# Six blocks instead of three by seven products of quarters, and side work in larger steps

## The chip, the cores and the metric

The program runs on one core of one Trainium2 chip. The metric is the device time of one execution in microseconds (us), the median of the runs shown. Beside it stands one profiled execution, whose span runs from its first to its last instruction. The engines are named as in the profile: PE is TensorE (matmuls), PEld its loads of the stationary operand, DVE is VectorE, ACT is ScalarE, POOL is GpSimd and SP is SyncE, which issues DMAs.

## What is computed

The input x has 4 sequences of 1024 tokens of 256 values, all in float32. Three layers follow one another:

```python
def ffn(x):                                   # weights w1 .. w3 hold -1, 0 and 1
    h = silu(lin(x, w1, s1)) * lin(x, w2, s2)       # 256 -> 1024
    h = gelu(lin(h, h1, s3)); h = gelu(lin(h, h2, s4))   # 1024 -> 1024, twice
    return lin(h, w3, s5)                           # 1024 -> 256
x = x + 0.5 * ffn(layernorm(x))
x = x + gelu(causal_convolution(layernorm(x), K)) @ W.T + b
x = x + 0.5 * ffn(layernorm(x))                # the same weights
```

K is a convolution kernel of 1024 taps for each of the 256 channels, computed from the inputs with exponentials, sines and cosines. The convolution goes over a Fourier transform of 2048 points.

## The kernel before

**Blocks.** The feed-forward network runs over 16 blocks of 512 tokens: f0 to f7 for the first application, g0 to g7 for the second. In a block there are first the two narrow layers w1 and w2 (64 matmuls of 512 columns, lines L382 and L383), then the two *wide* layers h1 and h2 (128 each, L415), then w3 (32, in `last_squares`, L630; in the last block in `last_tokens`, L658). An activation is split into a high and a low part (`fp32r`, a format of fewer bits that TensorE multiplies faster than float32), and the weights are whole numbers, so two matmuls make one exact product. The splitting costs a copy on ScalarE (L420) and a subtraction on VectorE (`low_part`, L309) for each tile.

**By quarters.** The last `N_BY_SUMS` blocks compute the wide layers in another way (`winograd`, L518). Both operands are cut into 2 x 2 quarters, and seven products of quarters take the place of eight, by the scheme of Strassen and Winograd. Each product is 32 pairs of stationary and moving tiles in `product` (L477) with 256 moving columns, twice for the two parts; so a wide layer is 224 matmuls of 256 columns. Sums and differences of activations are made on VectorE (`less`, `plus`), every operand is split (`operand`, L460), and the seven weight sums come from DRAM: `weight_sums` (L584) makes them once for both layers, in 16 parts of two VectorE operations each, and stores them. `load_slot` (L576) brings one of them, 1 MB, into one of four slots through SP's queue whenever a product is done. The slots take the SBUF space of the wide weights; so before the first such block all mixes and all parts of the weight sums have to be finished (L1285 to L1294: what is left of the sums is issued there in one go, and an assertion holds that the last mix is through).

**Side work.** Everything else runs beside the matmuls of the wide layers, given out in small steps by a generator, `all_aside` (L1225): the taps and their spectrum (`kernel_steps`, `kernel_spectrum`), then four *mixes*, m0 to m3 (`mix`, L1046), each the convolution of one sequence. Mix b needs blocks f(2b) and f(2b+1); blocks g(2b) and g(2b+1) need mix b. A mix has matmuls of its own on TensorE (L966, L1144, L1169). A second generator, `fillers` (L1244), holds the 16 parts of the weight sums and then 44 `weight_checks`: each loads 256 KB of weights again, compares them with -1, 0 and 1 (ScalarE's Sign for h1 and h2) or with the weights held, and counts misses; where one is found, a whole second version of the network runs, which it does not for these inputs.

**The counter.** `tick` (L1249) runs after each of the 16 output tiles of the wide layers but the last, 15 times in a block (in a block by quarters at 15 of 28 half products). It adds `STEP_WORK` (from f7's end on `STEP_WORK_2`) to an allowance and takes steps of `all_aside` until what they have issued reaches it. `counted` (L150) charges each of their VectorE operations `OP_WORK` = 130 plus its columns; a step without such an operation is charged `MIN_WORK` = 300. A step can also yield `PAUSE`: what comes next needs something that is still under way, so the tick ends there and the rest of its allowance is lost. At a pause one step of `fillers` is taken, if more than 642 of the allowance is left and `done` has more than eight entries (it has from f4 on). `prepare` (L1195) normalizes and transposes the next block's input in between; its VectorE operations are charged too, 4,900 in a block.

**Order on the engines.** Within these limits the instructions of an engine are put into an order when the program is built: the earliest written one that is ready comes first. A late operand at the start of a layer can thus be bridged by matmuls of the next output tiles. PSUM has eight tiles of a bank each (`psum`, L143), SBUF tiles of half a block come from a ring of 19 (`half`, L168), split operands from one of 15 (`ring`, L172).

Of the kernel before, what the change touches and what calls it, by code (L numbers as in the profile page):

```python
# [24 lines left out]
TB = 512  # L25
# [9 lines left out]

STEP_WORK, STEP_WORK_2, OP_WORK, MIN_WORK = 2500, 3000, 130, 300
PAUSE = "pause"
N_CHECKS = 44  # L40

N_BY_SUMS = 3
QT = TB // 2
QK = KH // 2
QW = HID // 2
# [62 lines left out]
def macaron_layers(  # L110
# [37 lines left out]
    work_done = 0  # L148
# [213 lines left out]
    def linear(ps, w, m, acts):  # L362
        n = len(acts)
        for k in range(n):
            for part in range(parts):
# [6 lines left out]
                )  # L372

    def ffn(xt, src, dst, blk, name, tick, ahead, final, by_sums):


# [21 lines left out]
        for layer, w in ((2, h1_sb), (3, h2_sb)):  # L398
            if by_sums:
                at = 0  # L400

                def step():
                    nonlocal at
                    at += 1
                    if at * KH // 14 > (at - 1) * KH // 14:
                        ahead()
                        if layer == 2 or at < 14:
                            tick()

                raw = winograd(raw, layer, name, step)  # L410
                continue
            hb = []
            for m in range(KH):
                ps = bank(f"p{layer}_{name}_{m}")
                linear(ps, w, m, ha)  # L415
                t = ring(f"h{layer}_{name}_{m}", parts, TB, dtype=wide)
                g = half(f"g{layer}_{name}_{m}") if split else t[:, 0, :]
                nc.scalar.activation(g, ps, AF.Gelu, scale=sc_sb[:, layer, m : m + 1])  # L418
                if split:
                    nc.scalar.copy(t[:, 0, :], g)  # L420
                    low_part(t, g)
                hb.append(t)
                ahead()
                if layer == 2 or m < KH - 1:
                    tick()
            ha = hb
# [91 lines left out]
    def winograd(raw, layer, name, step):  # L518
# [51 lines left out]
        (quarters[layer][i], f"w_{n}_{layer}_{i}")  # L570
        for n in range(N_BY_SUMS)
        for layer in range(2)
# [620 lines left out]
    done = []  # L1193
# [50 lines left out]
    fillers = chain(sums_of_weights, checks) if split else iter(())  # L1244
    late = late_pool = None
    ticks = 0
    allowed = 0

    def tick():  # L1249


        nonlocal ticks, allowed, work_done
        ticks += 1
        allowed = min(allowed, work_done) + (
            STEP_WORK_2 if ("f", n_blocks - 1) in done else STEP_WORK
        )
        while work_done < allowed:
            at = work_done
            if next(aside, PAUSE) is PAUSE:
                if len(done) > 8 and allowed - work_done > OP_WORK + TB:  # L1260
                    next(fillers, None)
                break
            if work_done == at:
                work_done += MIN_WORK
# [8 lines left out]
    allowed = work_done  # L1273
    for n, (turn, blk) in enumerate(blocks):
# [8 lines left out]

        by_sums = split and n >= len(blocks) - N_BY_SUMS
        if by_sums and not slots:  # L1285
# [93 lines left out]
```

## Time and profile before

| | us |
|---|---|
| median of 3 runs | 1400.81 (1399.09 to 1400.86) |
| the profiled execution | 1398.44 |
| its span | 1396.7 |
| TensorE busy / VectorE busy / ScalarE busy | 1384.2 / 932.8 / 766.8 |
| clock granted to TensorE, share of full speed | 0.999 |

The main groups of matmuls, by line (columns: line, engine, operation, output <- inputs, partitions x elements and how many; then busy us, mean ns of one, idle us of the engine before them):

| line | what | number | busy us |
|---|---|---|---|
| L366 | wide layers of 13 plain blocks (p_f, p_g) | 3328 of 512 columns | 768.4 |
| L366 | narrow layers of 16 blocks (pa, pb) | 1024 of 512 columns | 274.7 |
| L484 | wide layers of 3 blocks by quarters | 1344 of 256 columns | some 12.1 for each 96 |
| L630, L658 | w3 | 416 of 512 and 192 of 256 columns | 121.8 |
| L893, L966, L1144, L1169 | taps, spectra, mixes | | 115.2 |

A matmul's mean duration (391 ns for 512 columns) is longer than the distance to the next one (227 ns), since matmuls overlap; so distances and stretches of time are read here rather than durations. The same holds in a smaller way on VectorE, whose operations of 0.685 us overlap a little.

### The profile page before, as it was taken

To read this page: it belongs to the slowest core of one execution; us is meant where nothing else is said; L and a number is where in the kernel's file an instruction comes from. 1 tells how busy PE (TensorE), PEld (TensorE's weight loads), DVE (VectorE), ACT (ScalarE), POOL (GpSimd) and SP (SyncE) were. 2 spreads that over 40 slices of the span, in tenths; PEclk is the share of its full clock that TensorE was granted. 3 is DMA by queue.
4 is the path that set the end of the run, shared out by engine and by line. 5 is a ranking of instruction groups with operands and counts; after the bars stand their busy time and mean duration, and the time that the engine had idled before them with its cause. 6 is when DMAs were issued, how large, how long until landed. Compare 5 with 4: busy or idle time off the path is not lost.

```text
span 1396.7 us, 19695 instructions
## 1 busy us (share of the span) xinstructions
PE 1384.2 (99%) x7132; PEld 1182.6 (85%) x7132; DVE 932.8 (67%) x1766; ACT 766.8 (55%) x1227; POOL 297.0 (21%) x454
## 2 busy tenths in 40 slices
PE   9999999999999999999999999999999999999998
PEld 7888888888888888888888888888888888989998
DVE  6896667755637776377774569844597536877765
ACT  5986579644546445354353544534544445766664
POOL 4441022211312121521125301221112032121200
PEclk9999999999999999999999999999999999999999
DMA  9430101113131331532314414233132356959663
GB/s 355 127 131 21 41 16 46 31 30 96 50 108 36 106 90 54 203 92 83 76 46 162 134 37 128 61 91 106 53 95 50 100 143 237 332 169 320 193 221 114
DMA packets 121677, 160.11 MB, mean 115 GB/s; under 512 B 73873, under 2 KB 84113, under 8 KB 116193
## 3 DMA queue, kind: packets, MB, share of 16 engines
q1 hardware_dynamic: 99296, 99.41, 23.5%
q0 software_dynamic: 22000, 59.07, 13.7%
q8 instruction: 58, 0.95, 0.3%
q14 instruction: 51, 0.41, 0.1%
q10 hardware_dynamic: 272, 0.26, 0.1%
HBM read 120.95 MB, written 37.75 MB: 114 GB/s over the span
## 4 chain that ended last, share of the span: by engine, by line
PE 93%; DVE 3%; DMA 2%; ACT 1%; issue 0%; POOL 0%; SPq 0%; DVEq 0%; POOLq 0%; ACTq 0%
PE p_f L366 31%; PE p_g L366 19%; PE pa_f L366 4%; PE pa_g L366 4%; PE pb_f L366 4%; PE pb_g L366 4%; PE po_f L630 4%; PE po_g L630 4%; PE p2a_g L484 3%; PE p3a_g L484 3%; PE pi L1144 2%; PE pw L1169 2%; PE pf_m L966 2%; PE p2d_g L484 1%; PE p3d_g L484 1%; PE pk L893 1%
## 5 line engine op out<-in xcount | busy, mean ns | idle before, releaser
L366 PE MATMUL p_f<-h_f,h_sb 128*128 128x512 f32 x1024 | 237.1, 391 | 0.0
L366 PE MATMUL p_f<-ha_f,h_sb 128*128 128x512 f32 x1024 | 235.3, 390 | 0.0
L366 PEld LDWEIGHTS p_f<-h_f,h_sb 128*128 128x128 f32 x1024 | 191.8, 188 | 40.0 <-DVE h_f L309 0.3
L366 PEld LDWEIGHTS p_f<-ha_f,h_sb 128*128 128x128 f32 x1024 | 191.9, 188 | 39.8
L418 ACT ACTIVATE g_f<-p_f,sc_sb 128x512 f32<-128x512 f32 x128 | 87.7, 689 | 190.5 <-PE p_f L366 186.0
L309 DVE TENSOR_TENSOR h_f<-g_f,h_f 128x512 fp32r<-128x512 f32 x128 | 87.7, 689 | 143.3 <-ACT h_f L420 142.9
L418 ACT ACTIVATE g_g<-p_g,sc_sb 128x512 f32<-128x512 f32 x80 | 55.2, 690 | 174.6 <-PE p_g L366 165.0
L366 PE MATMUL p_g<-ha_g,h_sb 128*128 128x512 f32 x640 | 148.1, 391 | 0.0
L366 PE MATMUL p_g<-h_g,h_sb 128*128 128x512 f32 x640 | 147.9, 391 | 0.1
L366 PEld LDWEIGHTS p_g<-h_g,h_sb 128*128 128x128 f32 x640 | 120.0, 188 | 25.4 <-ACT h_g L420 0.5
L366 PEld LDWEIGHTS p_g<-ha_g,h_sb 128*128 128x128 f32 x640 | 120.0, 188 | 24.7
L309 DVE TENSOR_TENSOR h_g<-g_g,h_g 128x512 fp32r<-128x512 f32 x80 | 55.2, 690 | 111.8 <-ACT h_g L420 111.3
L339 POOL DMA_DIRECT2D moved<-sq_g x64 | 34.9, 552 | 314.9 <-DVE sq_g L156 313.8
L420 ACT CAST h_f<-g_f 128x512 fp32r<-128x512 f32 x128 | 78.3, 618 | 2.9
L418 ACT ACT_TABLE_LOAD x46 | 59.0, 1283 | 20.9 <-PE p_f L366 12.4
L366 PE MATMUL pa_f<-xt_f,w_sb 128*128 128x512 f32 x256 | 69.0, 390 | 0.7 <-DVE xt_f L321 0.7
L366 PE MATMUL pb_f<-xt_f,w_sb 128*128 128x512 f32 x256 | 68.8, 389 | 0.0
L366 PE MATMUL pa_g<-xt_g,w_sb 128*128 128x512 f32 x256 | 68.5, 389 | 0.0
L366 PE MATMUL pb_g<-xt_g,w_sb 128*128 128x512 f32 x256 | 68.4, 389 | 0.0
L392 DVE SCALAR_TENSOR_TENSOR g_g<-pb_g,sc_sb,g_g 128x512 f32<-128x512 f32 x64 | 47.7, 748 | 29.9 <-PE pb_g L366 19.2
L339 POOL DMA_DIRECT2D moved<-sq_f x56 | 30.8, 556 | 159.1 <-DVE sq_f L156 159.1
L392 DVE SCALAR_TENSOR_TENSOR g_f<-pb_f,sc_sb,g_f 128x512 f32<-128x512 f32 x64 | 47.3, 746 | 23.0 <-PE pb_f L366 15.9
(310 smaller groups left out, 2493.9 us busy)
## 6 DMA issues: line engine op xcount, KB each, us to landing
w<-q SPq DMA_DIRECT2D x42, 1024.0 KB, 6.1
q<-s POOLq DMA_DIRECT2D x40, 256.0 KB, 3.4
h_sb<-in_h_dram POOLq DMA_DIRECT2D x8, 1024.0 KB, 14.6
given<-in_h_dram SPq DMA_DIRECT2D x32, 256.0 KB, 5.0
kr<-k_hat SPq DMA_DIRECT2D x20, 256.0 KB, 2.7
ki<-k_hat SPq DMA_DIRECT2D x20, 256.0 KB, 2.9
xr_f<-in_x_dram SPq DMA_DIRECT2D x64, 64.0 KB, 2.5
q<-h_sb POOLq DMA_DIRECT2D x16, 256.0 KB, 5.8
```

The source lines that it names most:

```text
L309: return nc.vector.tensor_tensor(t[:, 1, :], src, t[:, 0, :].bitcast(F32), ALU.subtract)
L339: stores.dma_start(moved[k].rearrange("(c r) a q -> a r c q", r=SQ)[a], sq[a * SQ : (a + 1) * SQ].rearrange("r c j s -> r c (j s)"),)
L366: nc.tensor.matmul(ps, w[:, k, m * P : (m + 1) * P], acts[k][:, part, :], start=(k == 0 and part == 0), stop=(k == n - 1 and part == parts ...
L392: nc.vector.scalar_tensor_tensor(g if split else t[:, 0, :], pb, sc_sb[:, 1, m : m + 1], g, ALU.mult, ALU.mult)
L418: nc.scalar.activation(g, ps, AF.Gelu, scale=sc_sb[:, layer, m : m + 1])
L420: nc.scalar.copy(t[:, 0, :], g)
L484: nc.tensor.matmul(ps[:, e * QT : (e + 1) * QT], weights[:, c, m * P : (m + 1) * P], ops[c // 2][:, part, c % 2 * QT : (c % 2 + 1) * QT], ...
L630: nc.tensor.matmul(ps[:, n * n_t : (n + 1) * n_t], w3_sb[:, k, o * P : (o + 1) * P], act(k, part, n * n_t, (n + 1) * n_t), start=(k == ord ...
L893: nc.tensor.matmul(pk[0:NA, at + i, :, :].rearrange("p h b -> p (h b)"), a[:, i].rearrange("p a b -> p (a b)"), qd[d1 // per_tile][:, at + ...
L966: nc.tensor.matmul(ps[e][:, part, :], m[:, e, part, :], rows_of(q + JQ * e), start=True, stop=True)
L1144: nc.tensor.matmul(banks[dc][e][:, q * P : (q + 1) * P], vs[q + JQ * e][:, part, dc * P : (dc + 1) * P], m[:, e, part, :], start=(part == ...
L1169: nc.tensor.matmul(ps[:, e * D : (e + 1) * D], yts[dc][j // JQ][:, (j % JQ + e) * P : (j % JQ + e + 1) * P], wt_sb[:, dc, :], start=(dc == 0),
```

## The change

Three edits. `N_BY_SUMS` goes from 3 to 6: blocks g2, g3 and g4 are computed by quarters too, and everything that has to be through before the first such block, the last mix and the sums of the weights, has to be so before g2 instead of g5. The steps of side work become larger, 3600 for 2500 and 4000 for 3000. And at a pause up to two steps of `fillers` are taken, each under the same condition, instead of one.

```diff
-STEP_WORK, STEP_WORK_2, OP_WORK, MIN_WORK = 2500, 3000, 130, 300
+STEP_WORK, STEP_WORK_2, OP_WORK, MIN_WORK = 3600, 4000, 130, 300
...
-N_BY_SUMS = 3
+N_BY_SUMS = 6
...
             if next(aside, PAUSE) is PAUSE:
-                if len(done) > 8 and allowed - work_done > OP_WORK + TB:
-                    next(fillers, None)
+                for _ in range(2):
+                    if len(done) > 8 and allowed - work_done > OP_WORK + TB:
+                        next(fillers, None)
                 break
```

## The prediction

> **What bounds the kernel.** I read the page's busy shares and its chain of waits first, then busy time by stretches of time, one stretch per block of the feed-forward network.
>
> ```profile
> PE 1384.2 (99%) x7132; PEld 1182.6 (85%) x7132; DVE 932.8 (67%) x1766; ACT 766.8 (55%) x1227; POOL 297.0 (21%) x454
> ...
> PE 93%; DVE 3%; DMA 2%; ACT 1%; issue 0%; POOL 0%; SPq 0%; DVEq 0%; POOLq 0%; ACTq 0%
> ```
>
> TensorE is busy 1384.2 of 1396.7 us, and some 9 us of the rest are its start. So only two things move the end: fewer or shorter matmuls, or a new wait on TensorE. The stretches show both sides (start, length, then each engine's busy time with its instructions, clock, DMA share, GB/s):
>
> ```profile
> 9.20:89.60 80.40, 80.35 (x353) 66.04 (x354) 66.83 (x165) 67.01 (x91) 27.01 (x47) 1.00 0.72 231
> 89.60:176.00 86.40, 86.40 (x450) 71.65 (x449) 59.11 (x109) 52.09 (x89) 17.17 (x26) 1.00 0.13 31
> 440.90:520.70 79.80, 79.80 (x354) 66.09 (x353) 60.03 (x107) 38.05 (x56) 15.30 (x24) 1.00 0.33 90
> 795.50:882.60 87.10, 87.04 (x386) 71.97 (x384) 70.61 (x141) 41.43 (x62) 13.62 (x21) 1.00 0.31 85
> 1157.40:1237.60 80.20, 78.05 (x578) 73.97 (x577) 59.67 (x110) 56.26 (x107) 12.85 (x20) 1.00 0.81 283
> 1237.60:1313.80 76.20, 76.20 (x579) 73.52 (x579) 57.28 (x107) 50.67 (x96) 13.44 (x21) 1.00 0.73 241
> 1313.80:1390.00 76.20, 76.15 (x578) 73.43 (x576) 49.05 (x77) 48.23 (x91) 8.89 (x11) 1.00 0.45 157
> ```
>
> These are blocks f0, f1, f5, g1 and the three by quarters, g5 to g7. A plain block without side matmuls takes 79.8 us (f5), one by quarters 76.2 (g6, g7), and g5, the first of them, 80.2 because its TensorE stands still for 2.15 us. VectorE reaches 83% in f0 and 81% in g1 with no stall of TensorE.
>
> **Part 1: g2, g3, g4 by quarters.** Each exchanges 256 matmuls of 512 columns for 448 of 256 in the two wide layers, and 32 for 64 behind them. The wide layers alone, plain (f7) and by quarters (g6, g7):
>
> ```profile
> 636.00:694.00 58.00, 58.00 (x257) 48.06 (x256) 43.70 (x74) 22.13 (x34) 6.62 (x12) 1.00 0.33 90
> ...
> 1252.10:1306.10 54.00, 54.00 (x451) 53.83 (x450) 42.71 (x83) 39.65 (x77) 5.47 (x10) 1.00 0.84 291
> 1328.40:1382.30 53.90, 53.90 (x451) 53.90 (x450) 36.24 (x58) 37.33 (x74) 0.00 (x0) 1.00 0.57 205
> ```
>
> That is 4.0 us less there; the last layer gives back some 0.4 (64 narrow matmuls in 7.7 us against 32 wide ones in 7.3). Block against block: 79.8 - 76.2 = 3.6 us, three times **-10.8 us**.
>
> Here a rule of the Trainium skill stands against the row. "TensorE: Matmul & The Clock Gate", section "Back-to-back issue gap", gives N/2.4 + 2.5 ns for N columns: 215.8 and 109.2 ns, so 55.2 against 48.9 us, 6.3 saved per block and 18.9 in all. The section "LDWEIGHTS" of the same page speaks against that, and against the change: a stationary load costs columns/1.2, 107 ns for 128, about as long as a stream of 256, so nothing hides it. The rows side with the second: weight loads fill 53.90 of 53.90 us by quarters (48.06 of 58.00 before), and a step is 54.0/448 = 120 ns, not 109. I take 3.6 per block; no faster VectorE or DMA would improve it.
>
> The new blocks also add VectorE and ScalarE work. g7, nearly without side work, holds 49 and 48 us of 76.2, so both are covered. Each needs 14 weight parts of 1 MB, 184 GB/s over 76.2 us. g6 moved 241 GB/s with no stall, g5 283 with one; without the checks' loads the new blocks stay below g6. The first four parts cannot start before g1's last read of the wide weights, and have the last layer and the first one, some 22 us, until needed. g5 had the same start.
>
> **The stall in g5** (2.15 us by the row, 4.0 by the pitch) coincides with 15 weight checks there, whose DMAs share the rate above: on ScalarE the row of the sign operation waits 5.2 us for them in all, and the last layer waits for its operands:
>
> ```profile
> L630 PE MATMUL po_g<-hl_g,w_sb 128*128 128x256 f32 x128 | 16.6, 286 | 1.5 <-ACT hl_g L465 1.1 <-DVE hl_g L309 0.4
> ```
>
> After the change no check is left for these blocks (below). The gain is between 0 (a first block by quarters stalls anyway) and 4.0; I take **-3**, as g6 and g7 with few or no checks show none.
>
> **Part 2: larger steps.** The counter charges 130 plus its columns for a VectorE operation. 642 units are one 512-wide operation of 0.685 us (mean of the row of y<-y,z), 1.07 ns a unit; but operations in a row overlap by some 0.07 us, so in busy time it is less. At 0.94 f5's row (60.0 us, 37.5 thousand units with preparation) leaves 25 us for the block's own work, which is what its groups add up to (8 x 0.747 + 24 x 0.7 + two transposes and the input's split = 26). I take 0.94 and keep 1.07 as the upper end. I replayed the rule tick by tick over the unchanged list of steps: kernel taps and spectrum 129 thousand units, four mixes of 59, weight sums 16 x 1284, checks 44 x 642. Mix b still waits for f(2b+1). Units in thousands per block, without preparation (4.9 each):
>
> f0 33 to 49; f1 30 to 49; f2 34 to 34; f3 26 to 46; f4 26 to 36; f5 33 to 45; f6 33 to 44; f7 31 to 38; g0 30 to 50; g1 39 to 20; g2 to g7 together 100 to 0.
>
> The last mix ends at tick 144, six before g2's start at 150; the sums of weights are through in f6. So nothing is left to run in bulk at the exchange of pools. Nor does TensorE's side work grow: the same products come earlier.
>
> What grows is the load of VectorE and ScalarE. **f0:** VectorE 66.8 + 16.6 x 0.94 = 82.4 us against 80.4 of TensorE; **f1:** 59.1 + 19.3 x 0.94 = 77.2 against about 80 + 8 (half the tap products). **g0:** 25 + 55.1 x 0.94 = 77 (85 at 1.07) against 80 + 7 (forward products of mix 3). So f0 is over-full, f1 and g0 are nearly full, and f3, f5 and f6 lie below 93% at either price. ScalarE in f0:
>
> ```profile
> L418 ACT ACT_TABLE_LOAD x10 | 12.8, 1283 | 0.2
> ```
>
> That is ten reloads for Gelu in f0's wide layers (58.2 us), and as many for Exp, Sin and Sqrt. The first tap group's functions now all fall into f0: about six switches and four functions more. The Trainium skill, "ScalarE: Activation LUTs", section "What ACT_TABLE_LOAD costs", counts 1.28 us plus 1.38 of drain. By that six more switches cost 16 us, 86 of 80.4, and f0 would be late by 5 or more on ScalarE alone; the row shows 0.2 us of idle time before ten loads, so no drain, and I take 6 x 1.28 + 4 x 0.7 = 10.5: 67.0 + 10.5 = 77.5, nearly full.
>
> What of this reaches TensorE? In f0 of before the splits of h (L309) end up to 6.6 us after their matmuls and TensorE loses 0.1 us: the program's PE order fills in other matmuls while the last split is late. Ends: 0 if the excess drains in the 22 us without ticks that each block has; and the whole excess of the ticks, side + own split 0.69 + preparation against 3.63 us of matmuls and the side matmuls: f0 0.5 x 15 = 8 (14 at 1.07), g0 0 to 8, f3 0 to 3, f1 0 to 6. Sum 8 to 31. I take less than the lower sum, since f0 and f1 together need 160 of 168 us and each layer end tolerates 6.6: f0 3, f1 1, g0 1, **+5 us**.
>
> **Part 3: two fillers at a pause.** Same operations, only closer. A second check uses data whose load was issued just before; 3.6 us to landing (median, g0 to g4) can hold ScalarE, with Gelu behind it. Eight PSUM banks cover it except at a layer's end. A pair of weight sums queues seven stores of 0.55 us on POOL before the next block's squares; POOL is busy 21%. Between 0 and 5; I take **+1**.
>
> **Sum.** -10.8 - 3 + 5 + 1 = -7.8: span 1388.9, with the 1.7 us around it 1390.6 for the profiled run's 1398.4. The median shown lies 2.4 above that run: 1393.
>
> **Rivals.** A, *backlog reaches TensorE* (slower): VectorE's queue, f0 and g0 above all, is paid at layer ends. Price 8 to 31, taken 25, since it is a rival only at 1.07 ns a unit: 1400.8 - 13.8 + 25 = 1412; it decides once the stalls pass 14 us. For it: f0's 82.4 against 80.4. Against it: 81 to 83% cost nothing, and the full blocks have slack ones behind them. B, *a draw*: g2 stalls as g5 did and the stalls are near 11: 1400.8 - 10.8 + 11 = 1401, or 1398 to 1403. C, *no new wait*: 1400.8 - 13.8 = 1387. D, that three more blocks don't become cheaper, has g6 and g7 against it and I give it nothing.
>
> **Chances.** Forecast 0.59, A 0.21, B 0.13, C 0.07. 0.2% is 2.8 us, about what this measurement can tell: faster 0.66, same 0.13, slower 0.21. The range takes in C, the forecast, B and the edge of A: 1386 to 1405.
>
> **What would show it.** g3 to g7 at 76.2 us each; g2 at 76 (else the g5 stall was not the checks); TensorE's gaps in f0, f1 and g0 summing to about 5 us, ended by VectorE's splits or ScalarE; no checks after tick 144. Wrong if gaps beyond 14 us stand at layer ends, or if a tile that is not free holds Gelu up.

## The result and the profile after

| | before | after |
|---|---|---|
| median of 12 runs each, us | 1400.18 (1398.27 to 1401.11) | 1396.53 (1393.47 to 1400.46) |
| ratio, 95% interval | | 0.9975 (0.9967 to 0.9983) |
| the profiled execution / its span, us | 1398.44 / 1396.7 | 1396.3 / 1394.3 |

The change makes the kernel 3.65 us faster, of the 7.8 us that were forecast. The page of the changed kernel, its busy times and the first line of its chain of waits:

```profile
PE 1376.4 (99%) x7804; PEld 1205.9 (86%) x7804; DVE 1012.3 (73%) x1886; ACT 795.2 (57%) x1336; POOL 296.4 (21%) x454
...
PE 40%; DVE 3%; issue 0%; DVEq 0%
```

TensorE is busy 7.8 us less, by coincidence the sum that was forecast, but the span is only 2.4 us shorter: the difference is new idle time. The chain adds up to 43%, so it could be followed back over the last part of the program only; it is no ground for anything about the first half, where most side work is.

The stretches of the blocks f0, f1, g3 and g7 (start:end, length, busy time with instructions of PE, PEld, DVE, ACT and POOL, granted clock, DMA share, GB/s):

```profile
9.20:91.10 81.90, 81.86 (x352) 67.16 (x353) 72.89 (x169) 67.60 (x92) 29.19 (x51) 0.98 0.69 220
91.10:182.60 91.50, 89.79 (x482) 73.21 (x482) 76.97 (x137) 66.46 (x112) 15.48 (x24) 1.00 0.09 21
931.90:1007.80 75.90, 75.90 (x577) 73.41 (x576) 53.21 (x81) 48.35 (x92) 13.50 (x21) 1.00 0.79 270
1311.70:1387.80 76.10, 76.09 (x578) 73.37 (x576) 49.63 (x76) 48.23 (x91) 8.93 (x11) 1.00 0.46 157
```

The third line is one of the new blocks by quarters: 75.9 us, TensorE without a gap. The first two are the heavily loaded ones. (What the splitting is for shows in the distances of matmuls with 256 columns: 120 ns in `fp32r` by quarters, 216 ns in float32 in the mixes.)

**An account of the lost time.** Since busy time hides part of a stall (matmuls overlap), the loss is taken from starts: the distance between two matmuls in succession, less the usual distance of their kind (227 ns for 512 columns, 120 for 256), summed per block. Blocks with less than 0.9 in both are left out of the table.

| us lost | f0 | f1 | f2 | f3 | f4 | f7 | g0 | g1 | g5 | all blocks |
|---|---|---|---|---|---|---|---|---|---|---|
| before | 1.3 | 0.9 | 0.9 | 1.5 | 0.4 | 0.3 | 0.5 | 0.7 | 4.25 | 13.3 |
| after | 2.9 | 3.8 | 1.5 | 0.4 | 0.9 | 1.5 | 7.85 | 2.7 | 0 | 22.4 |

So the three blocks gave 10.8 or a little more, g5 gave back 4.25, and the other blocks took 13.4: -10.8 - 4.25 + 13.35 = -1.7, against -2.4 in the spans (with 79.8 - 75.9 = 3.9 us a block it is 11.7, and the sum -2.6). Of the new loss, 9.3 us lie in one place, the last layer of g0 and the start of g1's first layer. TensorE there, in the timeline (start, length, engine, line, operation; in brackets the idle time before and what ended it):

```profile
821.00 5.15 PE L630 MATMUL po_g<-h_g,w_sb 128*128 128x512 f32 x22
827.98 0.73 PE L630 MATMUL po_g<-h_g,w_sb 128*128 128x512 f32 x2 [1.83 <-DVE h_g L309]
829.41 1.22 PE L630 MATMUL po_g<-h_g,w_sb 128*128 128x512 f32 x2 [0.70 <-ACT h_g L420]
833.40 2.07 PE L630 MATMUL po_g<-h_g,w_sb 128*128 128x512 f32 x4 [2.77 <-DVE h_g L309]
```

The first 22 matmuls of w3 use tiles that are split already; the other ten come in small groups, whenever a split of h arrives. By starts the three waits are 2.0, 0.9 and 3.2 us, together 6.0. And the engines in stretches of 5 us through g0's second wide layer and its end:

```profile
786.00:791.00 5.00, 5.00 (x24) 4.14 (x23) 2.20 (x5) 1.31 (x2) 0.00 (x0) 1.00 0.56 149
796.00:801.00 5.00, 5.00 (x22) 3.86 (x22) 5.00 (x9) 2.83 (x5) 3.49 (x7) 1.00 0.33 85
806.00:811.00 5.00, 5.00 (x23) 4.13 (x23) 4.93 (x20) 3.42 (x6) 1.10 (x2) 1.00 0.69 220
816.00:821.00 5.00, 5.00 (x24) 4.13 (x22) 5.00 (x10) 1.74 (x4) 0.00 (x0) 1.00 0.41 125
826.00:831.00 5.00, 2.10 (x5) 0.80 (x4) 5.00 (x10) 1.89 (x3) 0.00 (x0) 0.76 0.00 0
831.00:836.00 5.00, 2.60 (x6) 1.66 (x6) 5.00 (x10) 2.01 (x3) 0.00 (x0) 0.50 0.53 84
```

The third busy number is VectorE: full from some 791 to 836 us, while ScalarE (the fourth) has 1.3 to 3.4 us in 5. So VectorE is behind. The splits of this layer end 5.1, 4.8, 11.0, 12.5, 13.4, 14.0, 15.8 and 15.0 us after the last matmul of their tiles, where before they ended 2.1 to 3.5 us after. From the third tile on, 7.4 to 10.5 us of this lie ahead of Gelu, which waits for VectorE to free a tile (below), and the rest behind it, in VectorE's own queue.

The two last lines also show a lower granted clock, 0.76 and 0.50 on average. In stretches that end where it changes, it is full, then half, then full again:

```profile
826.00:828.50 2.50, 0.67 (x3) 0.30 (x2) 2.50 (x6) 0.48 (x1) 0.00 (x0) 1.00 0.00 0
828.60:838.80 10.20, 6.74 (x15) 4.30 (x15) 9.80 (x23) 4.11 (x8) 0.00 (x0) 0.50 0.34 54
838.90:841.00 2.10, 2.10 (x11) 1.72 (x10) 2.10 (x6) 2.07 (x3) 0.36 (x1) 1.00 0.00 0
```

Twelve matmuls stand 400 to 600 ns apart in the middle stretch, which is 3.0 of the 9.3 us.

### The profile page after: what moved, and what is told of

Same layout as the page of the kernel before. It is cut to its first block, busy times and chain, and to the rows that moved or that the text cites. A ratio compares the mean times of both kernels' runs of the same rounds, so it can differ in the third digit from the quotient of the medians.

```text
span 1394.3 us, 21329 instructions
## 1 busy us (share of the span) xinstructions
PE 1376.4 (99%) x7804; PEld 1205.9 (86%) x7804; DVE 1012.3 (73%) x1886; ACT 795.2 (57%) x1336; POOL 296.4 (21%) x454
## 3 DMA queue, kind: packets, MB, share of 16 engines
q0 software_dynamic: 22000, 59.07, 13.5%
## 5 line engine op out<-in xcount | busy, mean ns | idle before, releaser
L366 PE MATMUL p_f<-ha_f,h_sb 128*128 128x512 f32 x1024 | 238.8, 392 | 0.1
L392 DVE SCALAR_TENSOR_TENSOR g_g<-pb_g,sc_sb,g_g 128x512 f32<-128x512 f32 x64 | 47.4, 746 | 29.4 <-PE pb_g L366 23.8
L391 ACT ACTIVATE g_g<-pa_g,sc_sb 128x512 f32<-128x512 f32 x64 | 43.6, 688 | 42.1 <-PE pa_g L366 41.9
L630 PE MATMUL po_f<-h_f,w_sb 128*128 128x512 f32 x256 | 60.7, 391 | 1.6 <-ACT h_f L420 0.9
L366 PE MATMUL p_g<-ha_g,h_sb 128*128 128x512 f32 x256 | 59.8, 392 | 0.0
L366 PEld LDWEIGHTS pa_f<-xt_f,w_sb 128*128 128x128 f32 x256 | 48.8, 190 | 12.2 <-DVE xt_f L356 1.0
L366 PE MATMUL p_g<-h_g,h_sb 128*128 128x512 f32 x256 | 59.1, 391 | 0.0
L630 PEld LDWEIGHTS po_f<-h_f,w_sb 128*128 128x128 f32 x256 | 47.6, 188 | 13.0 <-DVE h_f L309 2.0
L418 ACT ACTIVATE g_g<-p_g,sc_sb 128x512 f32<-128x512 f32 x32 | 22.1, 690 | 62.4 <-PE p_g L366 43.1
```

The lines of the kernel that those rows point to most:

```text
L366: nc.tensor.matmul(ps, w[:, k, m * P : (m + 1) * P], acts[k][:, part, :], start=(k == 0 and part == 0), stop=(k == n - 1 and part == parts ...
L391: nc.scalar.activation(g, pa, AF.Silu, scale=sc_sb[:, 0, m : m + 1])
L392: nc.vector.scalar_tensor_tensor(g if split else t[:, 0, :], pb, sc_sb[:, 1, m : m + 1], g, ALU.mult, ALU.mult)
L630: nc.tensor.matmul(ps[:, n * n_t : (n + 1) * n_t], w3_sb[:, k, o * P : (o + 1) * P], act(k, part, n * n_t, (n + 1) * n_t), start=(k == ord ...
```

## The experiments

The question was which part of the change makes this loss. The theories: **the step** (4000 units put more on VectorE in this layer than it can take beside the matmuls); **the pair of fillers** (a pair of checks put down at one pause blocks ScalarE or VectorE); **the ring** (VectorE is late with tiles of half a block, ScalarE's Gelu waits for one to come free, and this, not VectorE's own speed, makes the split late). A fourth, **the exchange** of memory pools before g2, could move the loss with the number of blocks by quarters.

**A smaller second step alone.**

```diff
-STEP_WORK, STEP_WORK_2, OP_WORK, MIN_WORK = 3600, 4000, 130, 300
+STEP_WORK, STEP_WORK_2, OP_WORK, MIN_WORK = 3600, 3000, 130, 300
```

> The changed kernel with the second step at 3000 instead of 4000 (first 3600, two fillers, six blocks). By the counter g0 then takes 39 thousand units instead of 50 and g1 31 instead of 20; the last mix ends at tick 148, still before g2. Theory 1 (VectorE is over-full in g0's second wide layer, and its backlog reaches TensorE there): the 9.8 us that TensorE loses at g0's end go, and the half clock behind them; time 8 to 10 us below the changed kernel, near 1387, ratio to before 0.990 to 0.992. Theory 2 (the pairs of checks hold ScalarE and VectorE): g0 and g1 keep five and six pairs, so at most a third of the loss goes, near 1393 to 1396. Theory 3 (Gelu waits for one of the 19 half tiles, which VectorE frees late): as theory 1, since with a shorter queue the tiles come free sooner; this run does not part the two.

(The 9.8 us there are an earlier count of the 9.3 above.)

Measured: 1392.01 against 1399.01, ratio 0.9956 (0.9942 to 0.9969). The loss at g0's end is 0.1 us. That is the step, and not the pair or the blocks, which were left as they are. It gained less than it removed, since the checks now reach into g1 (4.7 us lost) and a late split costs 1.4 us in g3. One wait in g1 is of a kind that I had not thought of. From the timeline of this kernel:

```profile
904.21 1.04 DVE L309 TENSOR_TENSOR h_g<-g_g,h_g 128x512 fp32r<-128x512 f32 x1 [3.38 <-ACT h_g L420]
...
907.83 0.69 DVE L309 TENSOR_TENSOR h_g<-g_g,h_g 128x512 fp32r<-128x512 f32 x1 [1.97 <-ACT h_g L420]
908.44 0.19 DVE L731 TENSOR_REDUCE total<-miss 128x1 f32<-128x44 f32 x1
...
908.78 0.19 PE L734 MATMUL p_bad<-ones,total 128*1 128x1 f32 x2 [2.35 <-DVE total L731]
```

The last step of the checks sums the misses by a matmul of one column. In TensorE's order it stands ahead of the layer's next matmuls, and TensorE stands still 2.4 us for it. VectorE isn't full there: it is idle for 3.4 and 2.0 us, since in its order two splits of h, each waiting for ScalarE's copy, stand ahead of the sum. Behind the wait the clock is at half for 3.4 us, and seven matmuls cost 1.4 us more; together 3.9 of g1's 4.7.

**One filler at a pause.**

```diff
-                for _ in range(2):
+                for _ in range(1):
```

> The changed kernel with one filler at a pause instead of two (steps 3600 and 4000, six blocks). g0's second layer keeps its 3852 to 5778 units a tick; some 24 checks move behind g1, into g2 to g4, one in a tick. Theory 1: g0's end still loses 8 to 10 us, time within 2 us of the changed kernel where g2 stalls by nothing, up to 4 us above it if g2 then stalls as g5 did before (checks and weight parts share the DMA rate). Theory 2: the loss at g0's end goes, 6 to 10 us below the changed kernel.

Measured: 1405.23 against 1399.01, ratio 1.0043 (1.003 to 1.0057), some 9 us slower than the change: a miss. The loss at g0's end stays at some 7 us, so a pair is worth at most some 2 of it. But with one filler at a time the checks aren't through before g2, and g2 loses 12.0 us. Its stretches (columns as above) and the waits around it (engine, output, line, what it waited for; us, times, longest):

```profile
960.00:975.00 15.00, 14.82 (x121) 14.35 (x119) 11.58 (x23) 10.37 (x23) 2.18 (x4) 1.00 0.93 301
975.00:990.00 15.00, 12.04 (x97) 11.62 (x96) 7.52 (x15) 7.01 (x13) 3.31 (x6) 1.00 0.94 343
990.00:1005.00 15.00, 10.47 (x66) 10.18 (x67) 11.12 (x21) 10.69 (x22) 0.00 (x0) 0.77 0.57 224
```

```profile
ACT sign L714 <- DMA given<-in_h_dram: 11.3, 4, 5.0
PEld p3a_g L484 <- ACT t3s_g L465: 5.3, 1, 5.3
```

The DMA engines are at 0.94, the checks' loads and the parts of the weights of the first block by quarters share them; ScalarE's sign waits 11.3 us for four of these loads, 5.0 for one. What stands behind it in ScalarE's order, and behind the comparison in VectorE's, comes late, and TensorE waits 5.3 us for its operand. g5's stall before was of this kind, a third as large.

**The blocks undone.**

```diff
-N_BY_SUMS = 6
+N_BY_SUMS = 3
```

> The changed kernel with three blocks by quarters as before: only the larger steps and the second filler. No gain from g2 to g4. Theory 1: the stalls of f1, f6 and g0 and the rest (some 14 us more than before) remain, and the 4 us lost in g5 before go, since no check is left there: time 8 to 11 us above before, ratio 1.006 to 1.008. If the stalls at g0's end come from the exchange of pools behind g1 or from the earlier weight parts, they are gone here and the time is 2 to 5 us below before.

Measured: 1405.86 against 1399.01, ratio 1.005 (1.0037 to 1.0064). Against the change's 0.9975 that is 0.75%, or 10.5 us for three blocks, where 10.8 were forecast. The loss at g0's end is 8.3 us with three blocks as well, with g2's start and its exchange far away; the exchange isn't the cause.

**One more tile in the ring, and its control.** The ring of 19 gets a twentieth tile. Two constants had to become narrower to make room for it, so the control has these alone.

```diff
-        return work.tile([P, *(shape or (512,))], dtype, tag="half", name=name, bufs=19)
+        return work.tile([P, *(shape or (512,))], dtype, tag="half", name=name, bufs=20)
...
-    miss = keep.tile([P, P], F32, name="miss")
+    miss = keep.tile([P, N_CHECKS], F32, name="miss")
...
-    eps = small.tile([P, 1 + 88], F32, name="eps", bufs=1)[:, 0:1]
+    eps = small.tile([P, 1], F32, name="eps", bufs=1)
```

> The changed kernel with 20 half tiles instead of 19 (the space comes from two constants that were wider than needed). Theory 3 (Gelu is held because no half tile is free): one tile more lets Gelu run further ahead of VectorE; g0's loss falls by a quarter or more, 2 to 5 us less. Theory 1 (VectorE's own rate; the waiting for a tile only passes it on): the split of h behind Gelu is as late as before, and the time stays within 1.5 us of the changed kernel.

> The changed kernel with the two narrower constants of d_half20 and 19 half tiles as before: the same instructions, only later SBUF addresses of the tiles behind them, not a multiple of what they were. d_half20's 512-column matmuls followed each other at 233 ns instead of 227 and it took 20 us more. If the addresses do that, the distance is 232 to 233 ns here too for the layers concerned, 15 to 28 us above the changed kernel, and its stalls say nothing against d_half20's reading. If the twentieth tile did it, the distance stays at 227 and the time is that of the changed kernel.

Measured: with 20 tiles 1415.98 against 1399.01, ratio 1.0117 (1.0102 to 1.0133); the control 1413.96 against 1399.7, ratio 1.0103 (1.0088 to 1.0119). Both are 18 to 20 us slower than the change, for a reason that has nothing to do with the ring (see the last section). But the stall can be compared: 8.8 us at g0's end with 20 tiles, 8.4 with 19, and the splits of the layer are late by the same 4.8, 4.7, 10.8, 12.2, 13.0, 13.5, 15.2 and 14.3 us in both. ScalarE's Gelu around that layer, in the change (797 to 828 us) and then with 20 tiles (815 to 850 us; groups: line, engine, operation, count, then busy us, mean ns, and idle before with what ended it):

```profile
L418 ACT ACTIVATE g_g<-p_g,sc_sb 128x512 f32<-128x512 f32 x6 | 4.1, 690 | 14.2 <-DVE z L156 6.7 <-PE p_g L366 4.3 <-DVE h_g L309 2.6
```

```profile
L418 ACT ACTIVATE g_g<-p_g,sc_sb 128x512 f32<-128x512 f32 x7 | 4.8, 689 | 13.3 <-DVE z L156 6.2 <-DVE y L156 4.9 <-DVE p_i L156 1.7
```

In both, Gelu is held up by VectorE's operations of the side work, the ones that free a half tile (z, y). So the ring does hand VectorE's lateness on to ScalarE (Gelu itself runs 7 to 11 us late in the change, 8 to 9 with 20 tiles), but one tile more changed nothing. I take it that with a full VectorE the next tile is used up as well; a much larger ring, which would show it, wasn't tried. What part of the delay a ring without limit would take away stays open.

**The second filler alone,** on the kernel before: smaller steps and three blocks by quarters as there.

> The kernel before with the second filler at a pause alone (steps 2500 and 3000, three blocks by quarters). The sums and the checks end before g5. If the checks made g5 stall, its 4.2 us go and nothing else changes: 3 to 5 us below before, ratio 0.9965 to 0.998. If a first block by quarters stalls whatever lies beside it, g5 keeps 3 us or more and the time is that of before. If pairs of fillers hold TensorE up where mixes run, new gaps stand in g0 to g4 and the time is above before.

Measured: 1393.52 against 1399.92, ratio 0.996 (0.9947 to 0.9973). This edit, whose parts I had put at +1 and -3, is worth 5.6 us by itself. Most of the gain is that the last check's Sign starts at 1125 us, before g5, whose stretch is now full; the losses of the other blocks stay as they were, 9.0 us in all.

```profile
1157.10:1233.10 76.00, 76.00 (x578) 73.50 (x577) 53.38 (x92) 51.93 (x95) 12.87 (x20) 1.00 0.71 246
```

**The change without the 44 checks.** This kernel leaves out the comparison of the weights; its flag is set to zero.

```diff
-    checks = weight_checks() if split else iter(())
+    checks = iter(())
...
+        nc.vector.memset(bad, 0)
```

> The changed kernel without the 44 checks of the weights (the flag is set to zero; fillers are the weight sums alone). Theory 1 (VectorE is over-full in g0's second wide layer by the steps of 4000): only one pair of checks lies in that layer, so g0's end still loses 6 to 10 us and the time is at most 4 us below the changed kernel. Theory 2 (checks): the loss at g0's end goes, 8 us or more below the changed kernel.

Measured: 1403.06 against 1399.92, ratio 1.0028 (1.0017 to 1.0039), a miss on the time. The matmuls of the wide layers stand 232 ns apart here and not 227, which for 2560 of them is about 13 us; so this time says nothing about the checks. The stall is a reading still: 6.4 us are lost at g0's end without a single check, 2.6 of them at half clock. The mix and its step suffice for most of it.

**The small second step, and the flag's matmul later.** On the first experiment, the matmul behind the checks is put five steps of filler later, so that its sum is ready.

```diff
-        yield
+        for _ in range(5):
+            yield
```

> Second step 3000 as in a_second3000, and the tiny matmul that adds up the misses of the checks five filler steps later than the reduction it reads (in a_second3000 TensorE stood still 2.4 us for it in g1). If that wait is a loss of its own, the time is 2 to 3 us below a_second3000, ratio to before 0.993 to 0.994; if g1 loses the same time elsewhere (its VectorE backlog), within 1 us of a_second3000.

Measured: 1387.54 against 1399.92, ratio 0.9924 (0.9908 to 0.994), the fastest of all, a further 0.3% below the first experiment. g1 loses 0.75 us now, g0's end 0.1. The same layer of g0 in this kernel:

```profile
782.00:797.00 15.00, 15.00 (x69) 12.57 (x68) 10.42 (x20) 6.03 (x11) 2.19 (x4) 1.00 0.29 88
797.00:812.00 15.00, 15.00 (x68) 12.43 (x67) 14.76 (x36) 7.30 (x10) 3.29 (x6) 1.00 0.55 176
812.00:829.00 17.00, 17.00 (x76) 13.86 (x75) 17.00 (x38) 10.04 (x14) 0.00 (x0) 1.00 0.45 109
```

VectorE is full in the last 30 us here as well, and TensorE has no gap. A full VectorE by itself is no loss here; its splits end at most 6.6 us late.

**A step between.** 3400 for the second step, else as in the last one.

> As h_late_flag (first step 3600, late flag matmul), with the second step at 3400. By the counter VectorE is given 26.3 thousand units in g0's second wide layer, against 28.9 at 4000 and 23.1 at 3000; what fits beside 29 us of matmuls and the layer's own splits (8 x 0.65 us) at 0.94 ns a unit is 25.3. Theory 1: g0's end loses between 0 and 3 us, time 0 to 3 us above h_late_flag. If the loss of the changed kernel had another cause in g0 (which h_late_flag moved by chance), it is either all there (8 us or more above) or all gone with the same chance.

Measured: 1389.59 against 1399.7, ratio 0.9925 (0.9912 to 0.9938), the same as with 3000. With it there are three doses. (The dose of 4000 has the flag's matmul in its old place; there it runs at 899 us, in g1, and nothing waits for it.) The units are what the counter charges in g0's second wide layer, with the next block's preparation:

| second step | thousand units in the layer | latest split, us behind its matmuls | lost at g0's end, us |
|---|---|---|---|
| 4000 (the change) | 28.9 | 15.8 | 9.3 |
| 3400 | 26.3 | 8.0 | 1.4 |
| 3000 | 23.1 | 6.6 | 0.1 |

Beside 29 us of matmuls (128 x 0.227) and the layer's own eight subtractions of some 0.65 us, VectorE has 23.8 us; at the prediction's 0.94 ns a unit that is 25.3 thousand units, an estimate that was on record before this run. The dose below it costs nothing, the one 4% above costs 1.4 us, the one 14% above 9.3.

**The first steps.** Two tries on the loss in f0 and f1, both on the best kernel: 3000 in f0 and f1 and 3800 in f2 to f7, and 3500 for all of f.

```diff
-STEP_WORK, STEP_WORK_2, OP_WORK, MIN_WORK = 3600, 3000, 130, 300
+STEP_WORK, STEP_WORK_2, OP_WORK, MIN_WORK = 3800, 3000, 130, 300
...
-            STEP_WORK_2 if ("f", n_blocks - 1) in done else STEP_WORK
+            STEP_WORK_2
+            if ("f", n_blocks - 1) in done or ("f", 1) not in done
+            else STEP_WORK
```

> As h_late_flag, with steps of 3000 in f0 and f1 as well and 3800 from f2 to f7. By the counter f0 takes 42 instead of 49 thousand units and f1 37 instead of 50; f3, f5 and f7 take 46, 52 and 44 instead of 46, 45 and 38. If the 3.8 us lost in f1 come from the taps' work being given out too fast there, some 2.5 to 3 us go: ratio to before 0.991 to 0.992, near 1387. If blocks of 50 thousand units cost 5 to 10 us wherever they are, as g0 did, f5 pays it instead: time 2 to 7 us above h_late_flag.

```diff
-STEP_WORK, STEP_WORK_2, OP_WORK, MIN_WORK = 3600, 3000, 130, 300
+STEP_WORK, STEP_WORK_2, OP_WORK, MIN_WORK = 3500, 3000, 130, 300
```

> As h_late_flag with the first step at 3500 instead of 3600 (f1 48 instead of 50 thousand units, f3 42 instead of 46, f5 48 instead of 45; the last mix still ends before g2). If the 3.7 us in f1 follow from its units, 0.5 to 1.5 us go and the time is 0 to 1.5 us below h_late_flag. If f5 at 48 pays as at 52 in g_early3000 (3 us), it is 1 to 3 us above.

Measured: 1401.73 against 1399.92, ratio 1.0019 (1.001 to 1.0027), and 1391.32 against 1399.7, ratio 0.9939 (0.9923 to 0.9954). The first is slower than the best kernel by nearly 1%, and a miss: f2 loses 8.9 us, 4.1 of it where tap products wait for VectorE, which neither forecast had. The second is 0.15% slower, within the intervals. f1 loses 5.2 us in the first and 8.0 in the second, against 3.7 with 3600.

But the places differ. f1's second wide layer in the change, with 3500 and with 3000 (columns as above):

```profile
144.10:173.30 29.20, 29.20 (x130) 24.16 (x129) 27.57 (x48) 27.81 (x36) 7.59 (x14) 1.00 0.14 37
145.30:174.40 29.10, 29.10 (x130) 24.06 (x129) 24.56 (x43) 27.15 (x33) 7.16 (x14) 1.00 0.13 37
143.70:177.30 33.60, 33.60 (x194) 27.92 (x193) 20.86 (x36) 24.68 (x43) 4.76 (x9) 1.00 0.22 48
```

The last split of the layer ends 8.7, 10.0 and 5.0 us behind its matmuls, and the w3 behind it loses 2.2, 3.5 and 0 us. So f1's end is a stall of g0's kind, and it goes where the layer is emptier; what the block was given in all did not tell it. But ScalarE is as full there as VectorE, with 3500 fuller, and which of the two sets the delay is not shown. With both edits 3.4 us are lost anew in f1's narrow layers.

## Why the prediction was wrong

**Right: Part 1.** g2 to g7 run at 75.9 to 76.1 us each, where 76.2 was taken, and three more blocks are worth 10.5 us by the experiment that undid them. The choice between the two estimates, the rows and the page's distance of 109 ns, went to the rows, and the distance measured in the new blocks is 120 ns again. (The page gives its formula for a single matmul, and in the same section lets loads and matmuls together set the distance in a stream; so its two sections did not contradict each other.) The bound on transfers was wrong: g3 moved 270 GB/s without a check, more than g6's 241 before, and TensorE didn't stall.

**Right: g5's stall.** It was the checks. With them through before the first block by quarters it is gone in the change (4.25 us recovered, 3 forecast) and with the second filler alone; with one filler it moves to g2 and grows to 12. The first block by quarters does not stall of itself. That it was their loads is seen in the waits of the run with one filler; a high rate alone, as in g3, is no stall.

**Near in sum, wrong in its working: f0 and f1.** 82.4 us of VectorE in f0 were worked out, 72.9 came. ScalarE has 67.6 there, not 77.5. Less side work falls into f0 than my replay of the counter had: in its wide layers there are eight loads of Gelu's table, ten before:

```profile
L418 ACT ACT_TABLE_LOAD x8 | 10.3, 1283 | 0.1
```

So the six more switches did not come, neither at my price nor at the page's price with a drain (0.1 us idle before eight loads). The overload that f0 was to have over its block never occurred; f1 got the 77 us of VectorE that were worked out, and in its second wide layer the full ScalarE that f0 was to have (27.8 of 29.2 us). f0 and f1 lose 1.6 and 2.9 us more than before where 4 were forecast; but 1.4 of f0's are in its narrow layers, ahead of all side work, where kernels with the same first block lost between 0.3 and 2.5 us. There the clock was at half from 9.4 to 12.8 us in the change and full before. So 3.1 are the change's, and the nearness of the sum is luck.

**Wrong: "g0 1", in Part 2.** That term was mis-sized: 9.3 us came. The step that failed is the one that made it small. First, the load was averaged over the block: 77 us of 80 + 7 looks nearly full, and it was taken as harmless. The block's sum was about right (VectorE was busy 79.5 us), but the work isn't spread over the block. 22 us of it have no ticks, and in the second wide layer 28.9 thousand units met room for 25.3. The place to compare them is one layer, since the layer behind it needs all its splits. Second, "each layer end tolerates 6.6" was right as a size (6.6 us late cost 0.1 with the step of 3000), but it was subtracted from an excess spread over blocks, and not compared with the up to 15.8 us by which this one layer was late. My own upper end for g0, 8 us for the excess of the ticks, was nearly the answer, and I argued it down. Third, the waits cost more than themselves: 3.0 of the 9.3 us are matmuls at half clock. I had no term for that. One sign that was named as one of being wrong came, too: a tile that wasn't free held Gelu up.

**Not seen: the cost in Part 3.** The second filler was priced at +1 for its bunching, with its benefit counted under g5's stall. Alone it brings 5.6 us, 4.25 of them g5's, and the other blocks lose no more than before. Beside the larger steps the bunching may cost something: one filler or no checks leave 7 and 6.4 of the 9.3, though both changed other things too. The part that I had not seen at all is the last matmul of the checks in TensorE's order; it costs nothing where it stands in the change, and 3.9 us with its half clock where the smaller step puts it.

Put together: -10.8 and -4.25 came as forecast or better; +6 of new stalls were forecast, 13.4 came. The rival "a draw" had the right size for them (near 11) but the wrong place (g2); "the backlog reaches TensorE" had the right mechanism and place (g0's layer end), though its price of 25 was twice too high; its point of decision, 14 us, was only just not reached.

Open: which engine makes f1's layer end late, the 1.7 us that f1 loses in small pieces in its first wide layer, and why nothing was put into the 2.8 us of 786 to 791 in which VectorE stood idle, waiting for ScalarE's copy, just ahead of the stretch in which it was behind (first stretch above).

## What to carry to other kernels

Side work that is given out in portions has to be compared with the engine's room between two deadlines (here one layer: its matmuls' time less the layer's own work on that engine), not with its share of a block: 9% under that room cost 0.1 us here, 14% over it cost 9.3 us. ScalarE has to be looked at in the same way, since at f1's end it was as full as VectorE. An edit that brings work forward can be worth its whole gain by what it gets out of the way of a later stage that is full of transfers, so look at where the work ends, not only at where it goes. The best version found is the change with a second step of 3000 (or 3400) and the flag's matmul put later, 0.9924 of the time before; of its ingredients the second filler gives 5.6 us on the kernel before and the three blocks some 10.5, and neither needs the larger second step.

## What the runs showed of the hardware

**The distance of matmuls changed when tiles were moved in SBUF.** Two constants made narrower, with the same instructions otherwise, changed the distance of all matmuls of 512 columns from 227 to 233 ns, and that of the 256-column ones of w3 from 120 to 113. In the control that is 3904 matmuls x 6 ns = 23 us, less 2 us from 320 of 256 columns. TensorE is busy 19.8 us longer (1396.2 for 1376.4); the medians show some 18, as 5 us less are lost in waits. The group of the wide layers, first in the change and then in the control:

```profile
L366 PE MATMUL p_f<-ha_f,h_sb 128*128 128x512 f32 x1024 | 238.8, 392 | 0.1
```

```profile
L366 PE MATMUL p_f<-ha_f,h_sb 128*128 128x512 f32 x1024 | 244.7, 397 | 0.0
```

The same count and shapes, 5 ns more on each. Without the checks the wide layers alone went to 232; a tile vanished there as well. Any experiment that changes a tile's size has to be read with the distance beside it. Which address makes the difference was not tried.

**One wait of 2 us was enough for half the clock, and a shorter one now and then.** At g0's end the clock is at half from 828.6 us, when only the first of the three waits, 2.0 us, has passed, and stays there for 10.2 us, through the other two. In g1 of the first experiment the 2.5 us between two matmuls at the flag were followed by 3.4 us of half clock. At f1's end waits of 1.1 and 0.9 us were followed by no half clock in the change; in the best kernel waits of 1.0 and 0.9 us were followed by this:

```profile
178.00:181.00 3.00, 1.40 (x5) 0.77 (x5) 2.93 (x8) 0.94 (x2) 0.00 (x0) 1.00 0.46 73
181.10:184.40 3.30, 3.30 (x9) 2.59 (x8) 2.42 (x5) 2.58 (x3) 1.27 (x1) 0.50 0.55 87
```

That is 1.6 us of f2's loss there, behind nearly the same waits; why in one and not in the other stays open. The Trainium skill, "TensorE: Matmul & The Clock Gate", section "HAM oscillation — how this bites in real kernels", warns of idle gaps above about 3.4 us; by that none of these waits would have been charged. The measurement decides: behind a wait of 2 us, count the matmuls that follow at twice their distance (3.0 us for twelve here), and behind one of 1 us, look.
